# The experts' shares of each token: products with a selecting matrix, or transfers through memory

## The chip, the core and the metric

The kernel runs on one core of a Trainium2 chip. The metric is the device time of one execution in microseconds, given as the median of a few runs. A core has five engines that work side by side, each with its own queue: TensorE (PE; its weight loads are shown apart as PEld), VectorE (DVE), ScalarE (ACT), GpSimd (POOL) and SyncE (SP), which here only starts transfers (DMAs). An engine takes its instructions in order, and one that waits holds back all behind it.

## The reference

The input x has 64 batches of 128 tokens of 128 values. Four steps follow each other, each added to its own input:

```python
x = x + _L0_xattn_ref(_layernorm(x), fside, ctx, ...)
x = x + _L0_ffn_ref(_layernorm(x), ...)
x = x + _L1_xattn_ref(_layernorm(x), ctx, ctx, ...)
x = x + _L1_ffn_ref(_layernorm(x), ...)
```

The change lies in the last. It has 8 experts with 64 inner rows each; every token goes to its best two:

```python
logits = xf @ Wg.T + bg
top_gates, top_idx = jax.lax.top_k(logits, 2)
top_gates = softmax(top_gates)
h = gelu(einsum('nd,erd->enr', xf, W1))
eout = SCALING * einsum('enr,edr->ned', h, W2)
sel = take_along_axis(eout, top_idx[:, :, None], axis=1)
out = sum(top_gates[:, :, None] * sel, axis=1)
```

The kernel computes all eight experts for every token (8 x 64 = 512 inner rows, in four columns of 128), multiplies each inner row by the token's share of that expert (its gate, or zero), and sums over the 512 rows in the second product.

## The kernel before

The 64 batches are handled in 16 groups of four (`GB`, `NG`). The kernel has three stretches by time: the first attention with the routing of the first experts (to about 620 us), the tiles of those experts (to about 1000 us), and the second attention with the last experts beside it (to the end). `attention(1, ...)` is a loop with one iteration per batch, and a tail. In an iteration come, in the order in which they are written: the products of probabilities and values of an earlier batch (L475, copy L484), the score products with their maxima (L407 and L430 on PE, reductions L414 on DVE, exponentials L438 on ACT), one piece of the last experts, half of the preparation of a later group (query products L292 with L295 and L301, keys L202 with L207, values L214), the steps that finish an earlier batch (L491 to L516), the router's steps (lines near L681 to L741), the shift of queries by the maxima (L459, L462), and gathers (L1360) and additions (L1372) on POOL.

The order of PE, ACT, DVE and POOL is that of the program's text (`tc.manual_schedule(engines=ORDERED)`, L16 and L1468). SP's queue is not in that set: the scheduler orders it. All products of the second attention go into eight PSUM banks that rotate (`mtile()`).

The last experts are a generator, `experts()` in class `Aside1`. Each iteration takes one piece of it (`aside.piece`, L599); what is left behind the loop is done by `aside.rest` (L615), which puts three steps of the router between pieces. A group has four pieces:

- piece 1: the gates of four batches (128 tokens by 4 x 32, of which 8 columns hold the experts) are transposed (L1413) and copied to `gT` (L1415), so that row 32j + e holds batch j's shares of expert e. Four products with the first weights (L1420), four Gelus (L1423) into `hT`: 128 rows by column c by 512 tokens. Row p of column c belongs to expert 2c + p // 64.
- piece 2: 32 products (L1430) of `select`, a matrix of zeros and ones, with a batch's rows of `gT` put each expert's shares on its 64 rows, in four banks; four multiplications (L1435) put them on `hT`.
- pieces 3 and 4: each 16 products with the second weights (L1441), an addition (L1446); the fourth ends with the store of 256 KB (L1448).

[...] Gelu and exponential have different tables, and each change is an ACT_TABLE_LOAD ahead of the first instruction that needs the other: before, ahead of L1423 in piece 1, and ahead of the exponential L438 of the following iteration.

Of the kernel before, what the change touches and what calls it, by code (L numbers as in the profile page):

```python
# [8 lines left out]
F32 = mybir.dt.float32  # L9
I32 = mybir.dt.int32  # L10
AF = mybir.ActivationFunctionType
ALU = mybir.AluOpType
# [6 lines left out]
GB = 4  # L19
NG = B // GB  # L20
S = 128
# [7 lines left out]
E = 8  # L29
# [15 lines left out]
def transformer_kernel(ctx, tc, a, out):  # L45
    nc = tc.nc

    const = ctx.enter_context(tc.tile_pool(name="const", bufs=1))
# [4 lines left out]
    for g in range(NG):  # L53
        t = resid.tile([S, GB, D], F32, name=f"x_{g}", tag=f"x_{g}")
# [17 lines left out]
    def load_const(name, shape, src):  # L72
        t = const.tile(shape, F32, name=f"c_{name}", tag=f"c_{name}")
        nc.sync.dma_start(t, src)
        return t
# [109 lines left out]
    for s in range(2):  # L185
        k = keep.tile([128, NV, GB, KF + KC], F32, name=f"k2_{s}", tag=f"k2_{s}")
# [598 lines left out]
    hbm = ctx.enter_context(tc.tile_pool(name="hbm", bufs=1, space=bass.MemoryType.DRAM))  # L785
    xs = hbm.tile([E * CAP, ROW], F32, name="xs", tag="xs")
    ys = hbm.tile([NTL * TT, D], F32, name="ys", tag="ys")
    place = ctx.enter_context(tc.tile_pool(name="place", bufs=1))
    at = place.tile([S, B, 2], I32, name="at", tag="at")
    posns = place.tile([S, 2, B], F32, name="posns", tag="posns")  # L790
# [532 lines left out]
    nc.sync.dma_start(row_number, a["row_number"])  # L1323
    steps256 = load_row("steps256", CAP // TT)
    tiles = load_const("tiles", [1, NA], a["tiles"])
    select = load_const("select", [128, 4, 128], a["select"])
    lw2 = load_const("lw2T", [128, 4, D], a["lw2T"].rearrange("(c p) d -> p c d", p=128))
    with tc.manual_schedule(engines=ORDERED):
        for _ in range(B - 2):
# [8 lines left out]
    class Aside1:  # L1338
# [65 lines left out]
        def experts(self):  # L1404


            for g in range(NG):
                while not self.ready:
                    yield
                of, gates = self.ready.pop(0)  # L1410
                assert of == g
                pt = self.mtile()[:, :S]
                nc.tensor.transpose(pt, gates.rearrange("p b e -> p (b e)"), ident)  # L1413
                gT = self.pool.tile([128, S], F32, name="gT", tag="gT", bufs=1)
                nc.scalar.copy(gT, pt)  # L1415
                xnT = self.xnTs.pop(g)
                hT = self.pool.tile([128, 4, GB * S], F32, name="h1", tag="h1", bufs=1)
                for c in range(4):
                    ph = self.mtile()
                    nc.tensor.matmul(  # L1420
                        ph, lhsT=lw1[:, c * 128 : (c + 1) * 128], rhs=xnT, start=True, stop=True
                    )
                    nc.scalar.activation(hT[:, c, :], ph, AF.Gelu)  # L1423
                yield

                pg = [self.mtile().rearrange("p (c t) -> p c t", c=4) for _ in range(GB)]
                for c in range(4):
                    for j in range(GB):
                        r = slice(32 * j, 32 * j + 32)
                        nc.tensor.matmul(  # L1430
                            pg[j][:, c, :], lhsT=select[r, c, :], rhs=gT[r, :], start=True, stop=True
                        )
                for j in range(GB):
                    h = hT[:, :, j * S : (j + 1) * S]
                    nc.vector.tensor_tensor(h, h, pg[j], ALU.mult)  # L1435
                yield
                for j0 in range(0, GB, 2):
                    po = self.mtile()[:, : 2 * D].rearrange("p (j d) -> p j d", j=2)
                    for j in range(2):
                        for c in range(4):  # L1440
                            nc.tensor.matmul(  # L1441
                                po[:, j, :], lhsT=hT[:, c, (j0 + j) * S : (j0 + j + 1) * S],
                                rhs=lw2[:, c, :], start=(c == 0), stop=(c == 3),
                            )
                    x = xg[g][:, j0 : j0 + 2, :]
                    nc.vector.tensor_tensor(x, x, po, ALU.add)  # L1446
                    if j0:
                        nc.sync.dma_start(  # L1448
                            out[g * GB : (g + 1) * GB].rearrange("b p d -> p b d"), xg[g]
                        )  # L1450
                    yield
# [21 lines left out]
def _laid_out(inp):  # L1473

    import numpy as np

    A = {k: np.asarray(v) for k, v in inp.items()}

    def moved(w):
        w = w.reshape(-1, NV, 4, 2 * HD)[:, ::-1]  # L1480
        return w.transpose(0, 2, 1, 3).reshape(-1, D)

    heads = np.arange(D).reshape(4, NV, 2, HD)
    hm, km, sm = (np.zeros((D, n), np.float32) for n in (NS, NV, NV))
    for v in range(NV):
        km[heads[:, 1 - v].ravel(), v] = 1.0
        sm[np.arange(4) * 32 + 16 * v, v] = 1.0
        for i in range(2):
            hm[heads[:, 1 - v, i].ravel(), 2 * v + i] = 1.0

    o = {"x": A["x"]}
    o["fsideT"] = A["fside_BxSxS_0"].transpose(2, 0, 1)
    c = A["ctx_1024"]
    o["ctxT"] = c.transpose(2, 0, 1)
    k = moved(c.reshape(B * KC, D)).reshape(B, KC, 1, D)
    o["ctx_k"] = np.where(km.T > 0, k, sm.T).transpose(3, 2, 0, 1)
    v = np.zeros((B, KC, H // 2, 2, 32), np.float32)
    for i in range(2):
        v[:, :, :, i, 16 * i : 16 * i + HD] = c.reshape(B, KC, H // 2, 2, HD)[:, :, :, i]
        v[:, :, :, i, 16 * i + HD] = 1.0  # L1500
    o["ctx_v"] = v.reshape(B, KC, H * 32).transpose(1, 0, 2)
    o["hmask"], o["kmask"], o["smask"] = hm, km, sm
    for p, l, names, tr in (
        ("a0_", "L0_xattn_", ("Wq", "bq", "Wk", "bk", "Wv", "bv", "Wp", "bp"), False),
        ("a1_", "L1_xattn_", ("W_q", "b_q", "W_k", "b_k", "W_v", "b_v", "W_o", "b_o"), True),
    ):
        wq, bq, wk, bk, wv, bv, wo, bo = (A[l + n] for n in names)
        if tr:
            wq, wk, wv, wo = wq.T, wk.T, wv.T, wo.T
        o[p + "wq"], o[p + "wk"] = moved(wq), moved(wk)  # L1510
        o[p + "bq"] = np.where(hm > 0, moved(bq).T, np.float32(0.0))
        if tr:
            o[p + "bqf"] = moved(bq).T
        o[p + "bk"] = np.where(km > 0, moved(bk).T, sm)
        o[p + "wv"], o[p + "bv"] = wv, bv
        o[p + "wo"], o[p + "bo"] = wo, bo
    o["wqkvT"] = A["L0_ffn_wqkv"].T

    w1 = np.zeros((E, D, 2, NF * 128), np.float32)
    w1[..., :F] = A["L0_ffn_w1"].reshape(E, 2, F, D).transpose(0, 3, 1, 2)  # L1520
    w2 = np.zeros((E, NF * 128, D), np.float32)
    w2[:, :F] = A["L0_ffn_w2"].transpose(0, 2, 1)
    w12 = np.concatenate(
        [w1.reshape(E, D, 2, NF, 128).transpose(0, 1, 3, 2, 4).reshape(E, D, NF, 256),
         w2.reshape(E, NF, 128, D).transpose(0, 2, 1, 3)], axis=3,
    )
    o["w12"] = w12.reshape(E, D, NF * 384)
    o["upper"] = np.triu(np.ones((128, 128), np.float32), 1)
    o["ones"] = np.ones((128, 128), np.float32)
    o["steps256"] = np.arange(CAP // TT, dtype=np.float32) * TT  # L1530

    t = np.zeros((4, 32, 4, 2, 64), np.float32)
    for e in range(E):
        t[:, e, e // 2, e % 2, :] = 1.0
    o["select"] = t.reshape(128, 4, 128)
    o["tiles"] = np.arange(NA, dtype=np.float32).reshape(1, -1)
    o["row_number"] = np.arange(1, 129, dtype=np.float32).reshape(-1, 1)
    o["first_row"] = np.arange(E, dtype=np.float32) * CAP
    o["wgT"] = A["L1_ffn_Wg"].T
    o["bg"] = A["L1_ffn_bg"]  # L1540
    o["lw1T"] = A["L1_ffn_W1"].transpose(2, 0, 1).reshape(D, E * R)
    o["lw2T"] = A["L1_ffn_W2"].transpose(0, 2, 1).reshape(E * R, D)
    return {k: np.ascontiguousarray(v) for k, v in o.items()}
# [18 lines left out]
```

## Time and profile before

| what | us |
|---|---|
| median of 3 runs | 1532.57 |
| lowest, highest | 1531.0, 1534.91 |
| the profiled execution | 1582.29 |
| its span, first to last instruction | 1580.5 |

The mean granted TensorE clock in the profiled execution was 0.973 of full speed. Times in the profile are those of this one execution, and a duration in it is not scaled to the median.

The busy shares in 40 slices of the span (each digit tenths, a slice 39.5 us) show the three stretches: the second attention begins near slice 26, and the last slices are its end and its tail.

```profile
PE   7969999999999999787999999888989898988987
DVE  6757888888888988354654444688776777777763
ACT  4646666666666666442333333566656565655653
POOL 4122345646465534464001122376555555444210
PEclk9989999999999999899999999899999999999999
```

The groups of instructions of the part that changes, in the stretch 960 to 1580 us; a row gives line, engine, operation, output and inputs, partitions by elements and count, then busy us and mean ns of one, then the engine's idle time just before them and what ended it:

```profile
L1441 PE MATMUL bank<-c_lw2T,h 128*128 128x128 f32 x512 | 64.8, 281 | 13.6 <-DVE nm L414 10.8 <-DVE h L1435 2.8
L1420 PE MATMUL bank<-xnT,c_lw1T 128*128 128x512 f32 x128 | 60.4, 616 | 3.6 <-DVE nm L414 3.6
L1423 ACT ACTIVATE h<-bank 128x512 f32<-128x512 f32 x64 | 35.6, 597 | 4.5 <-PE bank L1420 3.6
L1423 ACT ACT_TABLE_LOAD x15 | 19.2, 1283 | 1.7 <-PE bank L1420 1.4
L1415 ACT COPY gT<-bank 128x128 f32<-128x128 f32 x16 | 4.6, 289 | 7.3 <-PE bank L1413 7.3
```

A group takes four iterations, about 35.6 us in all. The iteration with piece 2 takes 9.6 us in groups of odd number and 11.1 to 11.5 us in those of even number up to the eighth; the even ones hold stretches of some 3 to 7 us in which PE was granted half clock.

### The profile page before, as it was taken

The page shows a single profiled execution, that of the slowest core. Times are in us where ns is not written, and L with a number is a line of the kernel's source. Part 1 is how long each engine was busy: PE and PEld are TensorE (multiplying, and loading weights), DVE is VectorE, ACT ScalarE, POOL GpSimd, SP SyncE. Part 2 cuts the span into 40 slices and gives each one's busy share as a digit, 9 for nine tenths or more (in the row PEclk, how much of TensorE's full clock was granted, in tenths as well). Part 3 has the DMA queues.
Part 4 walks back from the last instruction along what each step waited for, and adds up shares of the span by engine and source line. Part 5 has one row for each costly group of instructions (what it writes and reads, how often), then busy time and mean ns, then how long its engine had stood idle before and what let it go on. Part 6 is the DMA issues. An engine that isn't in the chain of part 4 may idle for free.

```text
span 1580.5 us, 41996 instructions
## 1 busy us (share of the span) xinstructions
PE 1442.8 (91%) x16620; PEld 1118.6 (71%) x16620; DVE 1106.3 (70%) x3024; ACT 849.7 (54%) x1740; POOL 641.3 (41%) x1195
## 2 busy tenths in 40 slices
PE   7969999999999999787999999888989898988987
PEld 5757777777777677676888888566666676666765
DVE  6757888888888988354654444688776777777763
ACT  4646666666666666442333333566656565655653
POOL 4122345646465534464001122376555555444210
PEclk9989999999999999899999999899999999999999
DMA  7851222222222221365776676111000111100000
GB/s 192 222 138 46 55 61 68 67 61 64 57 64 58 56 70 37 93 187 173 213 201 189 194 202 180 46 35 30 28 28 28 37 31 31 31 28 15 15 8 28
DMA packets 143719, 133.03 MB, mean 84 GB/s; under 512 B 48546, under 2 KB 126114, under 8 KB 141602
## 3 DMA queue, kind: packets, MB, share of 16 engines
q1 hardware_dynamic: 135330, 113.02, 25.9%
q0 software_dynamic: 8192, 17.32, 3.5%
q8 instruction: 132, 2.16, 0.6%
q14 instruction: 65, 0.53, 0.1%
HBM read 97.32 MB, written 32.97 MB: 82 GB/s over the span
## 4 chain that ended last, share of the span: by engine, by line
PE 66%; DVE 15%; DMA 6%; SPq 5%; issue 3%; ACT 3%; POOL 3%; another core or an unknown queue 0%; POOLq 0%; ACTq 0%; DVEq 0%
PE bank L430 10%; PE bank L475 9%; PE bank L1115 8%; PE bank L394 8%; PE bank L1420 4%; PE bank L1441 4%; DVE nm L414 3%; PE bank L1128 3%; DMA q<-xs 3%; SPq L1278 2%; PE bank L407 2%; PE bank L292 2%; DVE q L462 2%; PE bank L511 2%; PE bank L681 2%
## 5 line engine op out<-in xcount | busy, mean ns | idle before, releaser
L414 DVE TENSOR_REDUCE nm<-bank 128x2 f32<-128x496 f32 (+1 forms) x768 | 465.4, 662 | 100.6 <-PE bank L430 68.6
L438 ACT ACTIVATE p<-bank 120x512 f32<-120x512 f32 (+1 forms) x768 | 403.5, 603 | 154.9 <-PE bank L430 138.5
L430 PE MATMUL bank<-q,k 32*120 32x256 f32 (+1 forms) x3072 | 444.5, 401 | 14.8 <-DVE nm L414 5.0
L430 PEld LDWEIGHTS bank<-q,k 32*120 32x120 f32 (+1 forms) x3072 | 298.3, 182 | 61.9 <-DVE nm L414 16.6
L394 PE MATMUL bank<-k,q 32*128 32x248 f32 x2048 | 294.3, 403 | 12.5 <-DMA k<-in_ctx_k 11.8
L394 PEld LDWEIGHTS bank<-k,q 32*128 32x128 f32 x2048 | 203.1, 190 | 59.7 <-issue 23.0
L475 PE MATMUL bank<-p,v 128*32 128x128 f32 (+1 forms) x4096 | 179.6, 279 | 1.8 <-DVE h L1435 0.6
L1120 DVE TENSOR_TENSOR p<-p,bank 128x256 f32<-128x256 f32 x213 | 87.9, 420 | 125.4 <-ACT p L1119 112.6
L407 PE MATMUL bank<-k,qf 32*128 32x480 f32 x512 | 150.8, 604 | 1.3 <-ACT qf L295 0.8
L807 POOL DMA_INDIRECT xs<-xn,at x128 | 129.2, 1009 | 28.6 <-issue 25.0
L1119 ACT ACTIVATE p<-bank 128x256 f32<-128x256 f32 x213 | 80.9, 384 | 100.9 <-PE bank L1115 91.9
L484 ACT COPY ov<-bank 128x256 f32<-128x256 f32 x128 | 48.0, 375 | 157.5 <-PE bank L475 146.0
L475 PEld LDWEIGHTS bank<-p,v 128*32 128x32 f32 (+1 forms) x4096 | 111.2, 110 | 26.1 <-issue 13.2
L1115 PE MATMUL bank<-q 128*128 128x256 f32 x516 | 122.3, 388 | 4.6 <-ACT q L1106 4.6
L1360 POOL DMA_INDIRECT yb<-ys,back x112 | 108.7, 970 | 27.7 <-issue 19.3
L462 DVE SCALAR_TENSOR_TENSOR q<-bank,c_smask,q 128x256 f32<-128x256 f32 x256 | 111.1, 475 | 10.3 <-PE bank L459 9.6
L167 POOL TENSOR_SCALAR xn<-x,mv,rstd 128x128 f32<-128x128 f32 x252 | 110.6, 452 | 7.3 <-issue 1.3
L1115 PEld LDWEIGHTS bank<-q 128*128 128x128 f32 x516 | 97.4, 196 | 17.3 <-ACT q L1106 5.0
L155 POOL TENSOR_SCALAR rstd<-mv 128x4 f32<-128x4 f32 x32 | 6.4, 199 | 246.7 <-DVE mv L113 150.0
L475 PE MATMUL bank<-p,vc 120*32 120x128 f32 x2048 | 104.2, 272 | 0.6 <-issue 0.5
L1157 POOL DMA_INDIRECT kvT<-ys,back x16 | 15.4, 962 | 197.5 <-DMA vc<-xs 118.1
L301 ACT ACTIVATE q<-bank,c_a_bq,c_hmask 128x512 f32<-128x512 f32 x124 | 90.1, 788 | 9.8 <-PE bank L292 9.8
(224 smaller groups left out, 2477.6 us busy)
## 6 DMA issues: line engine op xcount, KB each, us to landing
q<-in_w SPq DMA_DIRECT2D x43, 576.0 KB
vc<-in_w SPq DMA_DIRECT2D x28, 576.0 KB
vc<-in_ctx_v SPq DMA_DIRECT2D x16, 960.0 KB
ys<-zero SPq DMA_DIRECT2D x71, 128.0 KB
k<-in_ctx_k SPq DMA_DIRECT2D x32, 240.0 KB
q<-xs SPq DMA_DIRECT2D x43, 128.0 KB
ys<-q SPq DMA_DIRECT2D x43, 128.0 KB
x<-in_x SPq DMA_DIRECT2D x16, 256.0 KB
```

The costliest lines, as they stand in the source:

```text
L167: nc.gpsimd.tensor_scalar(xn[:, j, :D], xg[g][:, j, :], self.mv[:, b, 0:1], self.rstd[:, b : b + 1], ALU.add, ALU.mult,)
L301: nc.scalar.activation(q4s[g][:, :, s, :], pq.rearrange("p (b q) -> p b q", b=GB), AF.Identity, bias=w["bq"][:, s : s + 1], scale=hmask[:, ...
L394: nc.tensor.matmul(pa[:, u, :], lhsT=q4s[g][r, j, s, :], rhs=k2[g % 2][r, s // 2, j, :], start=True, stop=True,)
L407: lambda: nc.tensor.matmul(pa, lhsT=qfs[g][r, j, :], rhs=k4s[g][r, :, j, :], start=True, stop=True),
L414: nc.vector.tensor_reduce(nm[b % 2].rearrange("q i (a s) -> q a i s", s=16)[:, 2 * ra + v : 2 * ra + v + len(slots) // 2, :, 0], pa.rearra ...
L430: nc.tensor.matmul(pb[:n, v * 256 : (v + 1) * 256], lhsT=k2[g % 2][r, v, j, k0 : k0 + n], rhs=q4s[g][r, j, 2 * v : 2 * v + 2, :].rearrange ...
L438: nc.scalar.activation(ps_[b][:n, c, ra, :], pb[:n], AF.Exp, scale=SCALE)
L462: nc.vector.scalar_tensor_tensor(q, pm, smask[:, v : v + 1], q, ALU.mult, ALU.add)
L475: nc.tensor.matmul(pav[32 * ra : 32 * ra + 32, v * S : (v + 1) * S], lhsT=vs[g % 2][c][:, j, 4 * v + ra, i, :], rhs=p[:n, c, ra, (2 * v + ...
L807: s = nc.gpsimd.indirect_dma_start(xs, bass.IndirectOffsetOnAxis(at[:, j, k : k + 1], 0), xn, None)
L1115: nc.tensor.matmul(ph[:, u, :], lhsT=w[:, c, u * 128 : (u + 1) * 128], rhs=xT, start=True, stop=True)
L1360: nc.gpsimd.indirect_dma_start(y[:, k, b % 2, :], None, ys, bass.IndirectOffsetOnAxis(back[:, b, k : k + 1], 0),)
```

## The change

The matrix `select` (256 KB, loaded at the start) and its 32 products per group go. Instead `gT` is written to DRAM (64 KB, two buffers in turn), and eight transfers read it back, each giving 64 partitions the same four rows (those of one expert, one per batch): 128 KB each, into the new tile `share` of the same layout as `hT`. `gT` itself now lies in a corner of `share`, in column 3, which the last transfers overwrite. The multiplications of piece 2 go by columns: two on POOL, two on DVE, both operands in SBUF. Behind the four Gelus an exponential of one element stands, on a tile that nothing else uses, so that the exponentials' table is loaded there.

On PE, 32 products per group are gone and all else keeps its order. On SP the write and the eight reads stand, in piece 1's place, ahead of the load of a later group's context (L256); for groups 14 and 15 the store L1448 of the group before stands between write and reads. On POOL the two multiplications stand between the gathers L1360 of one iteration and those of the next.

```diff
+    shares_ = [hbm.tile([128, S], F32, name=f"shares_{k}", tag=f"shares_{k}") for k in range(2)]
...
-    select = load_const("select", [128, 4, 128], a["select"])
+    again = const.tile([1, 2], F32, name="again", tag="again")
+    nc.vector.memset(again, 0.0)
...
                 nc.tensor.transpose(pt, gates.rearrange("p b e -> p (b e)"), ident)
-                gT = self.pool.tile([128, S], F32, name="gT", tag="gT", bufs=1)
+                share = self.pool.tile([128, 4, GB * S], F32, name="share", tag="share", bufs=1)
+                gT = share[:, 3, :S]
                 nc.scalar.copy(gT, pt)
+
+                there = shares_[g % 2]
+                nc.sync.dma_start(there, gT)
+                for i in range(2):
+                    for c in range(4):
+                        nc.sync.dma_start(
+                            share[64 * i : 64 * i + 64, c, :].rearrange("p (j t) -> p j t", j=GB),
+                            there.rearrange("(j e) t -> e j t", e=32)[2 * c + i]
+                            .unsqueeze(0).to_broadcast([64, GB, S]),
+                        )
...
                     nc.scalar.activation(hT[:, c, :], ph, AF.Gelu)
+
+                nc.scalar.activation(again[:, 1:2], again[:, 0:1], AF.Exp)
                 yield
-
-                pg = [self.mtile().rearrange("p (c t) -> p c t", c=4) for _ in range(GB)]
                 for c in range(4):
-                    for j in range(GB):
-                        r = slice(32 * j, 32 * j + 32)
-                        nc.tensor.matmul(
-                            pg[j][:, c, :], lhsT=select[r, c, :], rhs=gT[r, :], start=True, stop=True
-                        )
-                for j in range(GB):
-                    h = hT[:, :, j * S : (j + 1) * S]
-                    nc.vector.tensor_tensor(h, h, pg[j], ALU.mult)
+                    (nc.gpsimd if c < 2 else nc.vector).tensor_tensor(
+                        hT[:, c, :], hT[:, c, :], share[:, c, :], ALU.mult
+                    )
                 yield
```

More of the change, by code (lines that the diff above doesn't have):

```diff
@@ L1530, in _laid_out @@
     o["steps256"] = np.arange(CAP // TT, dtype=np.float32) * TT
[L1532 to L1535, printed above, removed]
     o["tiles"] = np.arange(NA, dtype=np.float32).reshape(1, -1)
```

## The prediction

> **What bounds the kernel now.** I read the first page of the profile: busy times, slices, the chain of the work that ended last.
>
> ```profile
> PE 1442.8 (91%) x16620; PEld 1118.6 (71%) x16620; DVE 1106.3 (70%) x3024; ACT 849.7 (54%) x1740; POOL 641.3 (41%) x1195
> PE 66%; DVE 15%; DMA 6%; SPq 5%; issue 3%; ACT 3%; POOL 3%; another core or an unknown queue 0%; POOLq 0%; ACTq 0%; DVEq 0%
> ```
>
> TensorE carries the chain, so fewer products look like a gain. But 91% is an average. Only the second attention (about 1000 to 1580 us) is touched, and there I read the groups of instructions:
>
> ```profile
> L438 ACT ACT_TABLE_LOAD x13 | 16.7, 1283 | 13.8 <-PE bank L430 9.9 <-PE bank L407 3.9
> L1435 DVE TENSOR_TENSOR h<-h,bank 128x512 f32<-128x512 f32 x64 | 39.7, 682 | 31.2 <-PE bank L1430 19.9 <-PE bank L491 11.1
> L1430 PE MATMUL bank<-gT,c_select 32*128 32x128 f32 x512 | 33.7, 302 | 12.6 <-ACT p L438 6.5 <-issue 4.1 <-DVE nm L414 1.5
> ```
>
> VectorE idles 31.2 us ahead of L1435, mostly for the select products; those wait for exponentials (by way of banks), and the exponentials for a table load. The timelines of group 1 (ScalarE, TensorE, VectorE) show one such place:
>
> ```profile
> 1157.69 1.28 ACT L438 ACT_TABLE_LOAD   x1 [0.75 <-PE bank L430]
> ...
> 1159.63 1.16 PE L1430 MATMUL bank<-gT,c_select 32*128 32x128 f32 x28 [0.37 <-ACT p L438]
> ...
> 1162.66 2.48 DVE L1435 TENSOR_TENSOR h<-h,bank 128x512 f32<-128x512 f32 x4 [2.81 <-PE bank L491]
> ```
>
> Behind the loop comes a tail with no attention left. Its chain:
>
> ```profile
> 1557.08 0.11 PE bank L1413
> 1557.19 3.44 PE bank L1420 x8
> 1560.62 1.18 PE bank L1430 x32
> 1561.81 0.70 DVE h L1435
> 1562.55 3.84 PE bank L1441 x32
> ```
>
> One group follows the other with TensorE nearly always busy. So the change meets two stages: a loop with cover, a tail without.
>
> **The gain in the loop.** 32 select products and four banks go from each of 16 groups. They run in four row groups at once: 1.16 us of PE in the row above, not 32 x 0.302. The exp table's load moves from L438 to just behind the Gelus; only 13 of 16 groups had one there, and group 15 gets a Gelu load back. The tail's loads lie beside longer waits: nothing. In odd groups (L295, the next table-free step of ScalarE, starts 1.7 us after the last exp) table 1.28 + select wait 1.7 = 3.0; I take off 0.5 for the moved load (1.28, plus a 1x1 exp of about 0.2), which now stands before oT's copy L506. In even groups the exps wait for products at half clock anyway; between 0 and 3.9 (table and the 2.0 before L295, and the wait between exps), taken 1.9. Five odd, five even, groups 10 and 11 together 3: 12.5 + 9.5 + 3 = **-25 us** (bounds -10 and -38). [...] Here the exp starts at 1158.98, right where the load ends (1157.69 + 1.28): [...] I keep the row's 1.28.
>
> **What the loop pays.** Let X be the end of the copy gT (L1415: 1149.65 in group 1). DVE reaches the multiply at X+10.2 in odd groups (1159.86, the end of L414's reductions) and near X+11 in even ones. The values now take a round trip through memory: SP issues the write (64 KB), its queue stands until that has landed, then eight loads of 128 KB. The row issues of this size are SP's constant loads, 0.43 us each every 0.47: 8 take 3.8. Small loads land 1.8 to 2.4 us after issue. The 1 MB is 2048 runs of 512 B, and each load reads only four rows, each 64 times. No row shows that. Nearest are these windows (columns: interval, us, PE, PEld, DVE, ACT, POOL busy, clock, DMA share, GB/s), the first with distinct rows, the second with two loads of one 512 B row to 128 partitions (c_a_bv, c_a_bo):
>
> ```profile
> 7.00:7.50 0.50, 0.50 (x2) 0.00 (x0) 0.00 (x0) 0.00 (x0) 0.50 (x1) 1.00 1.16 340
> 34.20:35.30 1.10, 1.10 (x19) 0.74 (x12) 1.10 (x2) 1.08 (x3) 0.00 (x0) 1.00 0.31 63
> ```
>
> At 340 GB/s 1 MB takes 3.1 us; at 55 (33.2 to 34.2 us) 19. Four rows at 55 each would give 220, 4.8 us. [...] I take 160, [...] since one row is nearest, so 6.5. Sum: 0.1 wake + 2.0 write landed + 1.0 first data + 6.5 + 0.5 completion = **X+10.1** (bounds 7 and 23). That just meets DVE's X+10.2: hidden in the loop. Past X+10 each microsecond stalls VectorE, whose queue holds out2's reciprocal, the shift, the next maxima, and TensorE waits for those: up to 12 us per microsecond over twelve groups.
>
> The multiplies: DVE's four from banks (0.68) become two on DVE; the row of such a product from SBUF (L1012) is 0.68 too. Two on POOL cost 1.27 each (L769). POOL idles for microseconds between its pairs of gathers, but stalls with them: gathers L1360 behind it are put off some 3 us, and the add L1372 has that slack. The two engines shut each other out: one L719 on VectorE, 0.22 us else, took 0.76 beside POOL's L1372 and ended with it. So 2 x 1.27 + 2 x 0.68 = 3.9 in series instead of 2.5. POOL's first two columns land two loads sooner, so I count 1.5 from the last landing to the down products. On SP the loads stand ahead of the context load kvT (L256, 3 us after X) and put it off some 6 us; the next keys (L207) were made at 1179, 25 us after its issue: nothing. The 256 KB select load goes, amid starting loads: nothing.
>
> **What the tail pays.** Groups 12 to 15 have no attention to cover the trip; the order by hand keeps the next group's products behind the down products L1441. Before, L1441 came 6.3, 6.6, 4.3 and 5.0 us after X (22.2). Now 10.1 + 1.5 = 11.6, call it 11.5: 46.0. Cost 23.8 us. TensorE then idles some 8 us in each, and before a 3.1 us gap was followed by half clock:
>
> ```profile
> 1542.50:1549.30 6.80, 6.08 (x15) 3.69 (x16) 2.11 (x13) 2.05 (x3) 0.42 (x1) 0.50 0.00 0
> ```
>
> L1420's eight took 4.99 there instead of 3.44 (+1.5). A down burst of 3.8 us at half clock costs about +2.5 by the same proportion: 4 x 2.5 - 1.5 = 8.5. Tail: **+32 us** (bounds +14: arrival at X+8.4 and no clock loss; +60: the slow rows' rate, partly under the four up products).
>
> **Sum.** -25 + 32 = +7 us on the profiled execution of 1582.3 (span 1580.5), giving 1589. That execution stands 3.2% above the median of the runs shown, 1532.6; I put the same +7 on it: **1540**.
>
> **Rivals.**
> (A) The forecast, loop hidden, tail open: 1540, own range 1530 to 1560; chance .46.
> (B) Repeated rows are slow: near 80 GB/s 1 MB takes 13 us, arrival X+16 or later. It decides from X+12. DVE then stands 5.8 us in each of twelve groups; less the 2.1 that a group gains and some 2 of slack that the maxima had, +1.7 x 12 = +20; the tail adds 4 x 6 to +32: 1532.6 + 20 + 56 = 1609. For it: 55 to 63 GB/s. Against it: those loads were two, overlapping issues at 0.4 us, perhaps not limited by the rows. Chance .14.
> (C) The other side, faster. One mechanism: the round trip is short. If rows flow at 300 GB/s, SP's eight issues set the end: 0.1 + 2.0 + 3.8 + 2.0 = X+7.9. Then nothing is late in the loop and even groups give their 3.9: -36, and the tail gives +20: 1517. It decides from a trip under about X+9 together with even groups over 3 us. For it: out_x's 256 KB went at 279 GB/s in its best half microsecond. Against: four rows[...]. Chance .23.
> (D) Both sums cancel within 0.3% (4.6 us, about what a measurement here can tell from no change): 1532, chance .17.
> That the change does not do what it says: TensorE's order loses exactly the 32 products a group and ScalarE's gains the load; only the trip's length is open.
>
> **Numbers.** Faster .23 (C), same .17 (D), slower .60 (A and B). The low end 1515 takes in C's time, the high end 1590 the lighter half of B.
>
> **What would show it.** Loads landing at X+10 with eight issues in 3.8 us; L1435's successor on DVE with no idle before it in the loop; intervals of the piece-2 iterations 2 to 3 us shorter (9.6 us in odd groups before); L1441 at X+11.5 in the tail with granted clock 0.5 in its bursts. Wrong if loads land at X+14 (B), or if the tail's L1441 starts before X+9 (C), or if the iterations keep their 9.6 us although nothing waits for the loads: then the table was hidden.

## The result and the profile after

The kernel after takes 1605.37 us (median of 4 runs, 1603.51 to 1611.52) beside 1532.88 us before: 1.048 times, 95% interval 1.0448 to 1.0512. The forecast was 1540, the range 1515 to 1590.

One thing has to be cleared first. The profile of before that the prediction read lasted 1580.5 us, and 1583 us turned out to be this kernel's ordinary time on some chips: in the experiments below, on several chips, it took 1534 to 1538 in three sets of runs and 1583 in two. I call these chips the first kind (chips 4 and 11) and the second (10 and 13). Only chip 11 stands in two sets, so that the chip, and not the occasion, makes the kind is likely but not shown. By its time the result was measured on the first kind; by its time and its intervals the profile that the prediction read is one of the second. So the kernel before was profiled once more on the first kind (1534.6 us), and the trace of after is compared with that one. The first lines of both pages, before:

```profile
PE 1422.9 (93%) x16620; PEld 1110.3 (72%) x16620; DVE 1102.3 (72%) x3024; ACT 846.9 (55%) x1740; POOL 640.4 (42%) x1195
PEclk9989999999999999999999999999999999999998
PE 67%; DVE 15%; DMA 5%; ACT 4%; POOL 4%; SPq 3%; issue 2%; POOLq 0%; ACTq 0%; DVEq 0%
```

and after:

```profile
PE 1442.4 (90%) x16108; PEld 1121.0 (70%) x16108; DVE 1099.7 (69%) x2993; ACT 854.2 (53%) x1759; POOL 683.6 (43%) x1227
PEclk9989999999999999999999998998999999999877
DMA packets 180693, 150.56 MB, mean 94 GB/s; under 512 B 50834, under 2 KB 163218, under 8 KB 178578
PE 59%; DVE 12%; DMA 11%; SPq 6%; POOL 4%; ACT 3%; issue 3%; POOLq 0%; ACTq 0%; DVEq 0%
```

512 products fewer, and TensorE is busy 20 us longer: the granted clock falls in the second attention and most in its last slices. Transfers and SP's queue have 17% of the chain instead of 8%. By the copies gT, the time up to the first group differs by 1.5 us, the twelve intervals that follow take 429.0 instead of 390.7 us (**+38**), and the tail behind the twelfth takes 86.2 instead of 53.2 (**+33**).

The loop, in group 2 after. SP's timeline, with the copy gT ending at 1161.9 (X, as in the prediction):

```profile
1161.91 0.32 SPq L1421 DMA_DIRECT2D shares<-share  x1
1163.48 5.20 SPq L1424 DMA_DIRECT2D share<-shares  x8
1168.78 0.97 SPq L256 DMA_DIRECT2D kvT<-in_ctxT  x1
```

The write had landed after 1.6 us, and the eight issues took 5.2 us, 0.65 each. The windows of the same stretch (us, five engines' busy time, clock, DMA share, GB/s):

```profile
1165.50:1166.00 0.50, 0.50 (x7) 0.50 (x6) 0.00 (x0) 0.48 (x2) 0.49 (x1) 1.00 0.28 45
1170.50:1171.00 0.50, 0.50 (x11) 0.16 (x3) 0.50 (x2) 0.50 (x2) 0.50 (x1) 1.00 1.09 218
1176.00:1177.00 1.00, 0.13 (x2) 0.13 (x2) 0.96 (x4) 0.19 (x1) 0.70 (x2) 0.91 0.11 33
1177.00:1178.00 1.00, 1.00 (x8) 0.92 (x10) 0.93 (x5) 0.00 (x0) 0.98 (x2) 0.50 0.12 33
```

In their first two microseconds of data the loads move 45 GB/s, although three to six of them have been issued by then; from 1167 on they move about 200. Their last packet starts at X+11.6. The lower two windows show the price. VectorE's and TensorE's timelines around them:

```profile
1173.99 1.95 DVE L1441 TENSOR_TENSOR h<-h,share 128x512 f32<-128x512 f32 x2 [1.42 <-DMA share<-shares]
1175.85 0.25 DVE L495 RECIPROCAL rs<-bank 128x16 f32<-128x16 f32 x1
...
1176.87 0.77 PE L430 MATMUL bank<-q,k 32*120 32x256 f32 x1 [1.98 <-DVE q L462]
```

In the kernel before on the first kind of chip, the same two places of the same group:

```profile
1166.85 2.48 DVE L1435 TENSOR_TENSOR h<-h,bank 128x512 f32<-128x512 f32 x4 [0.87 <-PE bank L1430]
...
1170.27 0.47 PE L430 MATMUL bank<-q,k 32*120 32x256 f32 x1
```

Follow the wait: the loads hold L1441, the queue of VectorE holds L495 and the shift L462 behind it, the shift holds TensorE for 1.98 us, and from there, and in the windows up to about 1183.5, TensorE runs at half clock. The first eleven groups of the loop have such gaps of 1.5 to 3.9 us ahead of L430, by the trace's matmul records, 3.0 on the mean, and the twelfth one of 5.6; in the kernel before on the same kind of chip no gap of TensorE in the first eleven exceeds 1.04, and the twelfth's is 1.6.

Over the twelve intervals, after first, then the kernel before with only the table moved (an experiment below), in the windows' columns:

```profile
1087.36:1516.35 428.99, 376.02 (x3794) 278.42 (x3793) 299.14 (x879) 249.48 (x486) 221.75 (x309) 0.90 0.26 57
1090.54:1473.18 382.64, 364.69 (x4178) 274.07 (x4177) 301.43 (x903) 248.73 (x486) 188.29 (x285) 1.00 0.11 29
```

TensorE stands idle for 53 us instead of 18, and is busy 11 us longer with 384 products fewer, at a mean clock of 0.90 instead of 1.00. So of the 46 us between the two, three quarters are idle time.

The tail after, from its chain:

```profile
1560.69 1.99 DMA shares<-share
...
1565.37 5.69 DMA share<-shares
1571.13 0.09 issue
1571.22 0.65 POOL h L1441
1571.88 0.57 issue
1572.44 1.27 POOL h L1441
1573.76 6.54 PE bank L1449 x30
1580.30 0.12 PE bank L1415
```

Where four lines of products stood, a trip stands. The first two of the 32 down products start at 1572.54, as soon as GpSimd's first column is done; the 30 behind them take 6.54 us, where all 32 took 3.84 before.

### The profile page after: what moved, and what is told of

The parts are those of the page before. It is cut to its first block, busy times and chain, and to the rows that moved or that the text cites. A ratio compares the mean times of both kernels' runs of the same rounds, so it can differ in the third digit from the quotient of the medians.

```text
span 1602.5 us, 41354 instructions
## 1 busy us (share of the span) xinstructions
PE 1442.4 (90%) x16108; PEld 1121.0 (70%) x16108; DVE 1099.7 (69%) x2993; ACT 854.2 (53%) x1759; POOL 683.6 (43%) x1227
## 4 chain that ended last, share of the span: by engine, by line
PE 59%; DVE 12%; DMA 11%; SPq 6%; POOL 4%; ACT 3%; issue 3%; POOLq 0%; ACTq 0%; DVEq 0%
PE bank L430 11%; PE bank L394 8%; PE bank L1116 8%; PE bank L475 7%; PE bank L1449 5%; DMA share<-shares 5%; PE bank L1129 3%; DVE nm L414 3%; SPq L1424 3%; DMA q<-xs 3%; PE bank L407 2%; SPq L1279 2%; DVE q L462 2%; ACT p L438 2%; PE bank L511 2%
## 5 line engine op out<-in xcount | busy, mean ns | idle before, releaser
L430 PE MATMUL bank<-q,k 32*120 32x256 f32 (+1 forms) x3072 | 454.4, 415 | 48.8 <-DVE q L462 41.9
L430 PEld LDWEIGHTS bank<-q,k 32*120 32x120 f32 (+1 forms) x3072 | 308.4, 189 | 99.1 <-DVE q L462 59.8
L407 PE MATMUL bank<-k,qf 32*128 32x480 f32 x512 | 175.1, 653 | 0.8 <-ACT qf L295 0.8
L475 PEld LDWEIGHTS bank<-p,v 128*32 128x32 f32 (+1 forms) x4096 | 109.6, 110 | 23.9 <-issue 13.1
L1449 PE MATMUL bank<-c_lw2T,h 128*128 128x128 f32 x512 | 87.9, 340 | 36.8 <-POOL h L1441 30.1
L1449 PEld LDWEIGHTS bank<-c_lw2T,h 128*128 128x128 f32 x512 | 80.3, 244 | 57.0 <-POOL h L1441 34.0
L1116 PE MATMUL bank<-q 128*128 128x256 f32 x516 | 118.7, 380 | 1.6 <-ACT q L1107 1.6
L462 DVE SCALAR_TENSOR_TENSOR q<-bank,c_smask,q 128x256 f32<-128x256 f32 x256 | 111.1, 475 | 8.6 <-PE bank L459 8.1
```

The source lines that it names most:

```text
L407: lambda: nc.tensor.matmul(pa, lhsT=qfs[g][r, j, :], rhs=k4s[g][r, :, j, :], start=True, stop=True),
L430: nc.tensor.matmul(pb[:n, v * 256 : (v + 1) * 256], lhsT=k2[g % 2][r, v, j, k0 : k0 + n], rhs=q4s[g][r, j, 2 * v : 2 * v + 2, :].rearrange ...
L462: nc.vector.scalar_tensor_tensor(q, pm, smask[:, v : v + 1], q, ALU.mult, ALU.add)
L475: nc.tensor.matmul(pav[32 * ra : 32 * ra + 32, v * S : (v + 1) * S], lhsT=vs[g % 2][c][:, j, 4 * v + ra, i, :], rhs=p[:n, c, ra, (2 * v + ...
L1116: nc.tensor.matmul(ph[:, u, :], lhsT=w[:, c, u * 128 : (u + 1) * 128], rhs=xT, start=True, stop=True)
L1449: nc.tensor.matmul(po[:, j, :], lhsT=hT[:, c, (j0 + j) * S : (j0 + j + 1) * S], rhs=lw2[:, c, :], start=(c == 0), stop=(c == 3),)
```

## The experiments

All are timed beside the kernel before on the same chip, so the ratio is what counts between kinds of chip.

| run | chip | us | times before (95%) |
|---|---|---|---|
| table moved alone | first | 1524.7 | 0.9931 (0.9906 to 0.9956) |
| the same, again | first | 1522.8 | 0.9911 (0.9880 to 0.9942) |
| the same, third time | second | 1581.7 | 0.9985 (0.9968 to 1.0002) |
| transfers in the loop, products in the tail | first | 1569.7 | 1.0233 (1.0204 to 1.0263) |
| the same, again | first | 1572.0 | 1.0224 (1.0192 to 1.0255) |
| products in the loop, transfers in the tail | first | 1556.0 | 1.0148 (1.0113 to 1.0183) |
| after, again | first | 1605.2 | 1.0438 (1.0398 to 1.0478) |
| after, third time | first | 1608.5 | 1.0472 (1.0447 to 1.0496) |
| after without the table's move | second | 1623.6 | 1.0277 (1.0237 to 1.0316) |
| after, multiplications on VectorE alone | second | 1618.1 | 1.0205 (1.0174 to 1.0236) |
| after, loads early and of other data | second | 1563.8 | 0.9886 (0.9852 to 0.9920) |
| after, long runs | second | 1589.6 | 1.0058 (1.0037 to 1.0080) |
| long runs, four loads | first | 1813.2 | 1.1809 (1.1774 to 1.1843) |
| long runs in the loop, products in the tail | first | 1546.9 | 1.0086 (1.0056 to 1.0116) |
| the same, again | second | 1565.1 | 0.9885 (0.9854 to 0.9917) |
| the same, VectorE alone | second | 1583.6 | 1.0009 (0.9992 to 1.0025) |
| the same, with unread products | second | 1571.6 | 0.9938 (0.9913 to 0.9962) |

### The change taken apart

First the kernel before once more, for its profile.

> The kernel before, unchanged, for a second profiled execution. Theory (the first profiled execution, 1582, was a slow one of its kind: half-clock windows that the runs at 1533 do not have): this one takes about 1533, its second attention (first gT copy to the end) about 443 us instead of 466.5, and its even groups lose the 11.3 us iterations. Rival (the profiler itself stretches this kernel): again about 1580 with the same windows.

It took 1534.6 us: the theory's time, with no half clock in the loop's groups; the copies gT are 32.5 and 34.0 us apart in turn instead of 35.6 and 35.9. The expectation's reason was wrong in one part: the first profile was no slow execution of its kind but looks like an ordinary one of the second kind of chip: the table run on chip 10 has nearly the same intervals (35.7 and 35.9).

Then the table's move alone, in the kernel before:

```diff
+    again = const.tile([1, 2], F32, name="again", tag="again")
+    nc.vector.memset(again, 0.0)
...
                     nc.scalar.activation(hT[:, c, :], ph, AF.Gelu)
+                nc.scalar.activation(again[:, 1:2], again[:, 0:1], AF.Exp)
```

> The kernel before with the exponentials' table moved behind Gelu and nothing else. Theory: the load was waited for in at most eleven groups at 1.28 us, so 1519 to 1530, faster by 3 to 14 us. Rival (the load now holds up the copies behind Gelu, oT above all): 1535 or more. Rival (the wait for the select products hides it anyway): within 3 us of 1533.

9.2 us gained. The copies gT are now 31.7 and 33.1 us apart: 0.8 to 0.9 a group, not 1.28. The repeats, one on each kind of chip:

> The kernel before with the table moved, again, beside the runs of this call. Theory: 6 to 12 us under the kernel before on any chip. Rival (worth only where the first such run was): within 3 us of before.

> The kernel before with the table moved, again, as the other base: both theories 0.988 to 0.996 times before.

On the first kind 12.2 us again; on the second nothing that can be told from no change, so the expectation that it helps on any chip was wrong.

Then the transfers in the loop and in the tail by themselves. Both kernels keep the table's move; the select matrix lies in the tile `share` where that has no other use.

```diff
-                share = self.pool.tile([128, 4, GB * S], F32, name="share", tag="share", bufs=1)
+                if g <= 12:
+                    share = self.pool.tile([128, 4, GB * S], F32, name="share", tag="share", bufs=1)
+                if g == 12:
+                    select = share[:, 0, :].rearrange("p (c q) -> p c q", c=4)
+                    nc.sync.dma_start(select, a["select"])
...
+                if g < 12:
...
+                else:
+                    pg = [self.mtile().rearrange("p (c t) -> p c t", c=4) for _ in range(GB)]
...
```

> The kernel after, with select products instead of transfers in the last four groups (the tail); the loop's twelve groups as after. Theory (loop and tail both lose: multiplications late by some 2 us in every loop group, and an open trip in the tail): the tail gives back about 34 us, 1571, and about 38 over before stay with the loop. Rival (the tail is all of it): about 1533 to 1540. Rival (the loop is all of it): about 1600.

> Select products in the first twelve groups, transfers in the last four only, the table moved in all. Theory: the table's run plus about 34, so 1555 to 1567. Rival (the tail is all of it): about 1600. Rival (the loop is all of it): about 1530.

Above the table run of the same set, the loop's transfers cost 1569.7 - 1524.7 = **45.0 us**, the tail's 1556.0 - 1524.7 = **31.4 us**. With the table's -9.2 that makes +67.2; the result is +72.5. The sum of the parts explains all but 5 us. The loop's case was run once more beside the kernel after:

> Short runs in the loop, products in the tail. Theory: 30 to 36 us under the kernel after on either chip, so within 0.6% of before where that takes 1583, 1.023 times before where it takes 1534. Rival (the tail costs more where the products are slower): less than 25 us under the kernel after.

36.5 us under after in the same set (1608.5): the tail's price again, with the 5 us that the sum of the parts leaves open. Behind a late loop the tail costs that much more than alone; why was not followed up.

### What makes the loop late

Two kernels took parts of after away: the table's move, and GpSimd's share of the multiplications (`nc.vector` for all four).

> The kernel after without the element's exponential, so that the table is loaded ahead of the next exponentials again. Theory (VectorE waits for the loads in the loop, so the table's move is hidden behind that wait): within 4 us of 1605. Rival (the move is worth the same 9 us as without transfers): about 1614.

> The kernel after with all four multiplications on VectorE, none on GpSimd. Theory (the loads' landing some 12.3 us behind the copy gT sets the end of the wait, not the two engines' lock nor GpSimd's stalled queue): 1595 to 1610. Rival (lock and stalled gathers are most of the loop's 45 us): 1580 or less.

They fell on a chip of the second kind, where after itself never ran, so neither tells how far it is from after: inconclusive. The traces are of use still: with VectorE alone the loads' last packet starts at X+11.1 to 13.7 in the loop (11.2 to 14.0 in after), so the landing was as late without GpSimd. When VectorE's multiplications begin (X+10.4 to 14.1) does not tell it there, since for most of them it came late by itself and found the loads landed.

Next the trip's lateness was taken away, with its traffic left, though at another time. This kernel leaves the experts' shares out of its result:

```diff
-                nc.sync.dma_start(there, gT)
...
-                            there.rearrange("(j e) t -> e j t", e=32)[2 * c + i]
+                            a["x"][g].rearrange("(j e) t -> e j t", e=32)[2 * c + i]
...
+                gT = hT[:, 3, :S]
+                nc.scalar.copy(gT, pt)
+                nc.sync.dma_start(shares_[g % 2], gT)
```

> The kernel after, but the eight loads of a group take the same pattern of rows from the input x, which no write precedes, and are issued as soon as the tile is free; the write of gT stays, and nothing reads it. So the experts' shares are left out of the result, and only the trip's lateness goes; bytes, runs, multiplications and the lock stay. Theory (lateness is the whole loss): loop and tail fall to the table run's level or below, 1505 to 1530. Rival (lock, stalled gathers, or the loads' traffic beside other transfers): 1545 or more.

18 us under before, on the second kind. The absolute figures of the expectation belonged to the other chip; as a ratio it is the theory's side. GpSimd's pair begins at X+9.3 to 9.4 in each of the first ten groups, which is GpSimd's own turn, and the tail's first down products at X+3.9 to 6.5.

Then one run of 2 KB for each partition instead of four of 512 B:

```diff
-    shares_ = [hbm.tile([128, S], F32, ...) for k in range(2)]
+    shares_ = [hbm.tile([32, GB, S], F32, ...) for k in range(2)]
...
-                nc.sync.dma_start(there, gT)
+                nc.sync.dma_start(there.rearrange("e j t -> j e t"), gT)
...
-                            there.rearrange("(j e) t -> e j t", e=32)[2 * c + i]
-                            .unsqueeze(0).to_broadcast([64, GB, S]),
+                            there.rearrange("e j t -> e (j t)")[2 * c + i].partition_broadcast(64),
```

> The kernel after, with the shares in DRAM ordered by expert first, so that each partition is filled by one run of 2 KB instead of four of 512 B; bytes, number of loads and partitions stay. Theory (the 2048 short runs make the trip long: the first load alone moved 45 GB/s, 44 runs in half a microsecond): the loads land 2 to 4 us sooner, the loop loses half of its 45 us or less, 1545 to 1580. Rival (64 partitions, the repeated reading of few rows, or the eight issues at 0.65 us set it): 1595 or more.

1589.6, on the second kind. GpSimd starts at X+9.3 to 10.3 in the loop's first ten groups (10.1 to 12.3 with short runs in after, on the first kind), and the tail's first down products at X+9.4 to 9.9 (11.0 to 11.9 in after). Group 2 in the timelines of GpSimd, VectorE and TensorE:

```profile
1192.89 2.49 POOL L1440 TENSOR_TENSOR h<-h,share 128x512 f32<-128x512 f32 x2 [0.47 <-issue]
...
1194.27 2.26 DVE L1440 TENSOR_TENSOR h<-h,share 128x512 f32<-128x512 f32 x2
...
1197.47 0.47 PE L430 MATMUL bank<-q,k 32*120 32x256 f32 x1 [0.18 <-issue]
```

Nothing waits for a DMA here, and the gap before L430 is 0.18 us. SP's eight issues were no faster (5.27 us), and the write, with its rows now in another order, landed a microsecond later (2.5 to 2.7 us after X instead of 1.6 to 1.8 in most groups of after): the runs, not the issues, made the landing late. VectorE's two multiplications take 2.26 us instead of 2 x 0.68 while GpSimd's second runs to 1195.38, as the lock that the prediction counted would have it.

Four loads over 128 partitions should have halved the issues:

```diff
-                for i in range(2):
-                    for c in range(4):
...
+                for c in range(4):
+                    nc.sync.dma_start(
+                        share[:, c, :],
+                        there.rearrange("e j t -> e (j t)")[2 * c : 2 * c + 2]
+                        .unsqueeze(1).to_broadcast([2, 64, GB * S]),
+                    )
```

> Long runs, and four loads over 128 partitions instead of eight over 64, in all groups. Theory (behind the runs, the eight issues of 0.6 us are next): landing 2 us sooner, the tail's down products near X+10 instead of X+12, so 8 us or more under the long-run kernel in the tail and nothing in the loop: on a chip where before takes 1583 about 1580, on one where it takes 1533 about 1540 to 1555. Rival (bytes or the receiving partitions set the landing): within 4 us of the long runs, 1590 or 1550 to 1565.

1813 us: far off on the other side of both. The columns land one after the other, over 5 us apart, as VectorE's timeline shows:

```profile
1157.32 0.69 DVE L1440 TENSOR_TENSOR h<-h,share 128x512 f32<-128x512 f32 x1 [12.22 <-DMA share<-shares]
1162.97 0.69 DVE L1440 TENSOR_TENSOR h<-h,share 128x512 f32<-128x512 f32 x1 [4.96 <-DMA share<-shares]
```

A window between them, with the five engines idle (the columns as above):

```profile
1149.00:1150.00 1.00, 0.00 (x0) 0.00 (x0) 0.00 (x0) 0.00 (x0) 0.00 (x0) 1.00 0.13 51
```

At 51 GB/s 256 KB take 5.1 us, and a share of 0.13 of 16 engines is the work of two. The source's outermost size is now 2 too, where the eight loads had 64. That the one follows from the other is the author's inference and was not shown: the partitions and the bytes of a load changed with it.

### A tail without transfers, and what is left in the loop

Long runs in the loop's twelve groups, products in the last four (the two edits above together):

> Long runs (one of 2 KB for each partition) in the loop's twelve groups, select products in the tail's four, the table moved. Theory (with the landing ahead of VectorE's turn, at X+9.3, and a tail without transfers, both losses are gone): at the level of the table run or up to 10 us below it, since 32 products a group are saved in the loop. Rival (GpSimd's multiplications and the lock cost what the products cost): 5 to 15 us above the table run.

> The long-run kernel with products in the tail, again, as the base of the two runs above: both theories 1.005 to 1.012 times before where before takes 1534, and less where it takes 1583.

1546.9 on the first kind, 24 us above the table run of its set, more than either side of the expectation had; 1565.1 on the second, 17 us below its table run. So long runs mend 23 us of the loop's 45 (1569.7 to 1546.9, in two sets with befores of 1533.9 and 1535.0), and the rest depends on the chip. What differs is the base. By the traces the loop's twelve intervals take as long on both kinds with long runs (396.1 and 393.7 us), but 382.6 and 414.3 in the table run, and 390.7 and 414.2 in the kernel before. (The other half of the 48 us between the two traces of before lies ahead of the first group, where the change does nothing.) The reason for the second kind shows in the table run there (TensorE, then VectorE, group 3):

```profile
1235.88 1.81 PE L1434 MATMUL bank<-gT,c_select 32*128 32x128 f32 x32
...
1240.27 2.48 DVE L1439 TENSOR_TENSOR h<-h,bank 128x512 f32<-128x512 f32 x4 [2.76 <-PE bank L491]
```

The products end at 1237.69, by a modelled end, and the multiplication begins 2.6 us later, as in each odd group up to the seventh; in the even ones up to the eighth the products themselves end some 2.8 us later than on the first kind, with half clock in the group. In the same kernel on the first kind it begins 0.1 us before that end, in every group of the loop:

```profile
1127.67 1.79 PE L1434 MATMUL bank<-gT,c_select 32*128 32x128 f32 x32
...
1129.36 2.48 DVE L1439 TENSOR_TENSOR h<-h,bank 128x512 f32<-128x512 f32 x4
```

So the same products cost more there, and taking them away gains what the table's move then cannot. In the odd groups of the kernel before there, the products end at X+11.1 and in the table run at X+10.4, yet the multiplication begins at X+13.0 in both: the wait took up what the table's move gave. What delays it is not settled. By the trace's semaphore updates, TensorE's signals to the other engines stand still for 3.0 us in these groups (1.3 in the table run on the first kind) and then come in a bunch, so it is TensorE's side that is late, not VectorE's. From group 9 on, in which GpSimd's last gather ends, the delay is gone there too.

Two kernels were to tell what eats the rest, the lock or TensorE's empty time: all multiplications on VectorE; and 32 products that nothing reads put back into piece 2.

```diff
+                    pf = [self.mtile().rearrange("p (c t) -> p c t", c=4) for _ in range(GB)]
+                    for c in range(4):
+                        for j in range(GB):
+                            r = slice(32 * j, 32 * j + 32)
+                            nc.tensor.matmul(
+                                pf[j][:, c, :], lhsT=lw1[r, c * 128 : (c + 1) * 128], rhs=xnT[r, :S],
+                                start=True, stop=True,
+                            )
```

> Long runs in the loop, products in the tail, all four multiplications on VectorE. Theory (the lock between GpSimd and VectorE stretches VectorE's part to the level of the products' four multiplications and beyond, and stalls GpSimd's gathers): 5 to 20 us under the same kernel with two on GpSimd. Rival (TensorE's idle time in the place of the products, and the half clock behind it): within 4 us of it.

> Long runs in the loop, products in the tail, and in the loop's piece 2 again 32 products of the same sizes, of other data into four banks that nothing reads. Nothing of the result changes; TensorE's work of the kernel before is back. Theory (the lock): 0 to 10 us over the kernel without them. Rival (TensorE's gaps and half clock are the loss): 8 to 20 us under it.

Both fell on the second kind. VectorE alone is 18 us slower: in spite of the lock GpSimd's share is worth having, and the theory of the lock falls there. The unread products cost 6.5 us on the medians (the intervals just touch), so TensorE's empty time is no loss there, and that rival falls too. But there the gaps ahead of L430 were no longer than 1.0 us in the first eleven groups to begin with. On the first kind they are up to 2.0, and neither kernel ran there, so for the 24 us on that kind both rivals stand. The trace of the long runs on that kind, taken in the fastest of the five runs (1538.7), shows 15 of the 24 us in the loop, and where they appear (TensorE, group 7 with long runs; up to group 9 the odd groups have such gaps of 1.5 to 2.0 us, the even ones of 0.9 to 1.3):

```profile
1341.11 0.47 PE L430 MATMUL bank<-q,k 32*120 32x256 f32 x1 [1.62 <-DVE q L462]
```

The table run has no gap there. TensorE arrives earlier by the products that it no longer makes, VectorE frees the shift no sooner (its multiplications end at X+13.0 instead of X+12.7), and three of the four odd groups from 1 to 7 take 36.0 to 36.5 us, with half clock inside (0.91 on the mean of group 1), where group 7 takes 34.2 at full clock and the table run 33.1. That describes the loss; that the half clock is its cause is argued, not shown.

After itself was run again with two of these sets, for the same base and to see it on the second kind:

> The kernel after, unchanged, beside the runs of this call, since the chips of the calls differ (the kernel before took 1533 in one, 1583 in another). Theory: where the kernel before takes 1533, 1605 again; where it takes 1583, whose loop is slower by 23 us of waits between TensorE and the others that the change partly removes, about 1615, 1.02 times before. Rival (one ratio everywhere): 1.048 times before on both.

> The kernel after, unchanged. Theory (on a chip where before takes 1583 the change saves the products' longer wait, some 2 us in each loop group, and pays the same for the trip): 1.012 to 1.025 times before there, and 1.044 to 1.048 where before takes 1534. Rival (the same ratio on every chip): 1.044 to 1.048.

Both fell on the first kind: 1.0438 and 1.0472. What the change does on the second was not measured.

Of all these, the table's move alone is the version that beats both kernels on the chip of the result, by 0.7 to 0.9%; long runs with products in the tail do on the other kind (1.2%) and lose on the first.

## Why the prediction was wrong

- **The step that failed: the 6.5 us for 1 MB (160 GB/s) in the sum "X+10.1. That just meets DVE's X+10.2: hidden in the loop."** The 160 GB/s was the author's estimate, between the rows of 55 and 340 GB/s; the trace read then has no loads of this form. The 0.1, 1.0 and 0.5 us beside it were estimates too. Up to the first data the sum was right: 3.1, and measured in after X+3.0 to 3.2 in ten of the twelve loop groups (in group 2 the write took 1.6 us instead of 2.1 with the wake, the first data 1.4 instead of 1.0). But the last packet starts at X+11.2 to 14.0: the megabyte took 8.2 to 10.4 us. (The 0.5 behind it held in group 2: X+11.6 to VectorE's X+12.1.) So GpSimd's pair starts at X+9.7 to 12.3, VectorE stands 1.0 to 3.8 us ahead of its own (0.1 in the table run), and its last multiplication ends at X+13.4 to 16. With one run of 2 KB for each partition the megabyte took 5.6 to 6.9 us on the same kind of chip (152 to 187 GB/s), which is the forecast's term; whether the 64 partitions bound it there, no run tells. (Issues of 0.65 us, 5.2 in all instead of 3.8, were no term of that sum.) A sum without slack was booked as no cost, although the text itself said what each microsecond past X+10 costs. The loop was forecast at -25 and came out at -9 + 45 = +36.
- **"Less cover" was priced as a delay alone.** In the tail the prediction counted half clock behind an idle TensorE; in the loop it did not, and there each late group left a gap of some 3 us with half clock behind it.
- **The select wait of 1.7 us,** the other half of the gain, came from the first profile and is seen on that kind of chip only, as is the half clock of the even groups. On the chip of the result the multiplication starts as the products end, so there was nothing of it to gain. The profile's own time, 3.2% above the runs shown, was the sign: it was carried over as an offset, when it meant that some waits in the trace were not those of the runs.
- **The table** was sized at up to 1.28 us in eleven groups, some 14 of the 25. Alone it gave 9 to 12 on the chip of the result, and nothing that can be told from no change on the kind of the profile.
- **The tail's number was right, in part by luck.** Forecast +32 us; measured +31.4. The down products were to start at X+11.5, and the first two did at 11.6, 11.2, 11.9 and 11.0. But the last landing came a microsecond later than X+10.1 (last packet at X+11.1 and 11.2 in groups 12 and 13), and the 1.5 us behind it were too many, since the first products need only GpSimd's first column; the other thirty start at 12.8, 12.4, 13.1 and 12.2. Half clock was forecast at +2.5 a burst: these thirty take 6.2, 6.5 and 5.5 us in three of the four, where 32 took 3.84.
- **Rival B had the right direction** and nearly the time (1609), by a wrong division: it gave 20 us to the loop and 56 to the tail, where the traces have 38 and 33. Its mechanism, a late landing that decides from X+12, is what was seen, but its size was not: slow repeated rows did not reach X+16. The long runs read the same rows as often and were in time (GpSimd's start on the first kind at X+9.2 to 9.8 in the first ten groups, against 10.1 to 12.3), so the count of short runs was the cause, not the repetition.

## What to carry to other kernels

A transfer that replaces work on an engine has to land with slack before the consumer's turn in its queue; a sum that meets it to 0.1 us is a forecast of a stall, and what is queued behind the consumer pays: here 45 us in twelve groups. Take a transfer's rate from loads with its own length of run, and place the runs in memory so that each partition takes one: here 1 MB took 5.6 to 6.9 us in runs of 2 KB and 8.2 to 10.4 in runs of 512 B. Where a profile's execution is some per cent off the runs to be predicted, find the stage that differs before its waits are priced.

## What was not expected of the hardware

- The chips differ for this kernel by 3% (1533 to 1538, and 1583), and by the sign of an edit: long runs with products in the tail 1.0086 and 0.9885 times before.
- Loads of 256 runs of 512 B moved 45 GB/s in their first two microseconds of data and about 200 after that; eight loads in which each partition takes one run of 2 KB were issued no faster and moved the megabyte in 5.6 to 6.9 us instead of 8.2 to 10.4.
- Loads of 256 KB to 128 partitions, from a source with an outermost size of 2, moved 51 GB/s at a DMA share of 0.13; which of these sizes did it was not shown.
- TensorE made 512 products fewer and was busy 20 us longer: half clock stood behind its gaps (0.50 from 1177 to 1183 in group 2), and the loop's mean clock fell from 1.00 to 0.90.
- In the table run on the second kind of chip TensorE's signals stand still for 3.0 us around the select products of odd groups up to the seventh; the same kernel has 1.3 us on the first kind.
